# A four-layer graph network on a sparse matrix: diagonal terms moved from TensorE to ScalarE and VectorE, the short block first, column sums in the middle of layer 1

## The chip, the core and the metric

The kernel runs on one core of a Trainium2 chip. Its engines are TensorE (PE, matrix products; PEld are its weight loads), VectorE (DVE), ScalarE (ACT), GpSimd (POOL) and SyncE (SP), each with its own instruction queue that is worked off in order. The metric is the device time of one execution in microseconds (us).

## The reference, cut to what matters

x is 2708 x 512, adj is 2708 x 2708 and sparse: about four entries a row beside the diagonal, which is always there. Four layers follow each other, each in the form x = layernorm(x + layer(x, adj)):

```python
# layer 0
layer0 = (x - (adj @ x) * (diag + 1)) @ W0 + b0
# layer 1: gates ga, gb = sigmoid([adj @ x, x] @ Wa.T + ba), the same with Wb, bb
h = x @ W_sa
e = where(adj != 0, exp(-leaky_relu(s_left + s_right)), 0)
attn = e / (sum(e, axis=1) + 1e-5)
layer1 = sigmoid(ga * (attn @ h) + gb * (adj @ (x @ W_gc) + b_gc))
# layer 2: head = (adj > 0) / norm of its rows
inc = adj + head
layer2 = (inc @ x) / sum(inc, axis=1)
# layer 3: A = adj + I, deg = column sums of A, d = deg ** -0.5
layer3 = tanh((d[:, None] * A * d[None, :]) @ x @ W3.T + b3)
```

## The kernel before, in words

The 2708 nodes make 22 blocks of 128 rows; the last one, block 21, has 20 rows. Layer 0 reads adj once, block by block, and finds the entries beside the diagonal of every 128 columns (at most 8 in a segment of some blocks). It turns them into a list of edges: a full block has 5 tiles of 128 edges, the short one 1 tile (TILES, `n_tiles`). What is kept of them is ev (values, with the diagonal's value behind the last tile), ej and er (the node at either end), and pick, a 0/1 matrix per tile that says which row of the block an edge belongs to. A dense path stands behind a flag and isn't taken here.

Each later layer aggregates a block like this: GpSimd gathers the 5 x 128 neighbour rows from DRAM with indirect DMAs (L599, one per tile, tile xg, two buffers, in layer 1 also sl, a few columns of the row's own node). Then TensorE sums them up (`aggregate`, L656). A tile can be summed in two ways:

- *As an f32 product:* VectorE multiplies pick by the edge values (`weighted_edges`, L620), and TensorE multiplies the result with xg.
- *Split:* ScalarE scales the gathered rows by the edge values into a rounded fp32r tile hi (L641), VectorE computes the remainder lo (L643), and TensorE multiplies pick with hi and with lo. The rings of hi and lo have n_parts buffers each.

SPLIT_A, SPLIT_E and SPLIT_3 say how many of the 5 tiles are split in layer 1's two sums and in layer 3's; the others go as f32 products, and layer 2 splits none. The first product of every aggregate is the diagonal term: ScalarE scales the identity by the diagonal's values (`weighted_diagonal`, L629), and TensorE multiplies it, f32, with the block's own rows xs.

Layer 1 has two aggregates a block, l1a (by adj) and l1e (by the attention's weights). Its finish scales them by the gates into ua (L1213) and ue (L1215) on ScalarE, transposes both on TensorE (L679), copies them to SBUF on ScalarE (L684), and projects them with two weights into one accumulator, 8 f32 products (L692). Then follow L1222 on VectorE, a tanh on ScalarE (L1226), the residual (L1227), the norm (with a square root by Newton steps on VectorE, L718 to L737, and the scaling on ScalarE, L740), and the store to DRAM. Layer 3's finish scales its aggregate on ScalarE (L1360), transposes, projects with 4 products, and goes on in the same way from L1365; layer 2's has no projection (L1324).

Layer 0's order is written out by hand (`steps`, `plan`): each step has a time within a block, and blocks follow each other every 15.81 planned us, by block number. Outside it the tile framework orders the instructions of each engine from the program's order and its own cost model; `layer` gives the program's order as gather(i+1), prepare(i+1), then compute(i), with finish(i-1) between l1a and l1e. A layer's first gather reads rows that the layer before stored, so it waits for that layer's last store.

Ahead of layer 1 stand the column sums of adj for layer 3 (L1255 to L1279): a loop over five blocks of VectorE rows over 128 x 880 elements, some small rows, and a Sqrt on ScalarE (L1275). Behind layer 1 stands a second Sqrt, for layer 2's row norm (L1286). In layer 2 the prepared weights are two VectorE passes (L1310, L1318) over 6 x 128 columns: five tiles and the diagonal.

Of the kernel before, what the change touches and what calls it, by code (L numbers as in the profile page):

```python
# [12 lines left out]
P = 128  # L13
# [427 lines left out]

SPLIT_A, SPLIT_E, SPLIT_3 = 5, 3, 4

# [44 lines left out]
def sparse_path(  # L488
# [18 lines left out]
    def rows(i):  # L507
        return P if i < NF else TAIL

    def n_tiles(i):  # L510
        return TILES if i < NF else 1

    keep = outer.enter_context(tc.tile_pool(name="keep", bufs=1))
# [76 lines left out]
    d_inv = const.tile([P, NB], FP, name="d_inv")  # L590
    dd3 = const.tile([P, NB], FP, name="dd3")
    vsum = const.tile([P, NB], FP, name="vsum")
# [34 lines left out]
    def weighted_diagonal(s, i, v):  # L627
        r = rows(i)
        nc.scalar.activation(s[:, n_tiles(i), :r], ident[:, :r], AF.Copy, scale=v)  # L629

    def weighted(i, vals, pool, name, diag=None, first=0):
        nt = n_tiles(i)
        s = pool.tile([P, TILES + 1, P], FP, tag="s", name=name)
        weighted_edges(s, i, vals, first)
        weighted_diagonal(s, i, vals[:, nt : nt + 1] if diag is None else diag)
        return s
# [11 lines left out]
    def picked(pool, i):  # L648
# [5 lines left out]
        return s  # L654

    def aggregate(pool, i, s, tiles, tag, name, pick_s=None, parts=()):  # L656

        r = rows(i)
        nt = n_tiles(i)
        agg = pool.tile([P, D], FP, tag=tag, name=name)  # L660
        products = [(s[:, nt, :r], xs[:, i, :D])]
        products += [(s[:, t, :r], tiles[:, t, :D]) for t in range(len(parts), nt)]
        products += [(pick_s[:, t, :r], x_) for t, pair in enumerate(parts) for x_ in pair]
        for k, (w, x_) in enumerate(products):
            nc.tensor.matmul(  # L665
                agg[:r, :], lhsT=w, rhs=x_, start=k == 0, stop=k == len(products) - 1
            )
        return agg
# [45 lines left out]
    def rsqrt(y, a, r, name):  # L714

        k = small.tile([P, 4], FP, tag="newton", name=f"nw_{name}")
        bits = small.tile([P, 1], U32, tag="bits", name=f"bits_{name}")
        nc.vector.tensor_scalar(  # L718
            bits[:r, :], a.bitcast(U32), 1, None, op0=ALU.logical_shift_right
        )  # L720
        y0, t, y1, q = (k[:r, j : j + 1] for j in range(4))
        nc.vector.tensor_scalar(
            y0.bitcast(U32), bits[:r, :], -1.0, float(GUESS), op0=ALU.mult, op1=ALU.add
        )
        nc.vector.scalar_tensor_tensor(t, y0, a, y0, op0=ALU.mult, op1=ALU.mult)
        nc.vector.scalar_tensor_tensor(t, t, -10.0 / 3.0, t, op0=ALU.add, op1=ALU.mult)
        nc.vector.scalar_tensor_tensor(y1, t, 5.0, y0, op0=ALU.add, op1=ALU.mult)
        nc.vector.scalar_tensor_tensor(q, y1, a, y1, op0=ALU.mult, op1=ALU.mult)
        nc.vector.scalar_tensor_tensor(q, q, -64.0 / 3.0, y1, op0=ALU.add, op1=ALU.mult)
        nc.vector.tensor_scalar(y, q, -27.0 / 1024.0, None, op0=ALU.mult)  # L730

    def layernorm(dst, v, r, name):
# [355 lines left out]
    )  # L1088
    plan = [(i * STEP + s[0], i, s[1], s[2:]) for i in range(NB) for s in steps]
    plan.append((40, 0, lambda i: score_weights(), ()))  # L1090
    with tc.manual_schedule():
        for _, i, step, more in sorted(plan, key=lambda e: e[:2]):
            step(i, *more)

# [39 lines left out]

    n_parts = 9

# [5 lines left out]
    def l1_prepare(i, tiles):  # L1142
# [50 lines left out]

        g = w1p.tile([P, 3], FP, tag="g", name=f"g{i}", bufs=3)
        nc.vector.tensor_add(g[:r, 0:2], sums[:r, 3:5], xs[:r, i, D + 4 : D + 6])
# [5 lines left out]
        nc.vector.reciprocal(g[:r, 2:3], g[:r, 2:3])  # L1201
        nc.vector.tensor_mul(g[:r, 2:3], g[:r, 2:3], g[:r, 0:1])
        na, ne = min(nt, SPLIT_A), min(nt, SPLIT_E)
        parts_a = [split_rows(w1p, tiles, t, ev[:, i, t : t + 1], f"a{i}") for t in range(na)]
        parts_e = [split_rows(w1p, tiles, t, e[:, 2, t : t + 1], f"e{i}") for t in range(ne)]
        sv = weighted(i, ev[:, i], spool, f"s1v{i}", first=na)
        se = weighted(i, e[:, 2], w1p, f"s1e{i}", first=ne)
        return sv, se, g, picked(w1p, i), parts_a, parts_e

    def l1_finish(i, g, agg_a, agg_e):  # L1210
        r = rows(i)
        ua = work.tile([P, D], FP, tag="u", name=f"l1ua{i}")
        nc.scalar.activation(ua[:r, :], agg_a[:r, :], AF.Copy, scale=g[:r, 1:2])  # L1213
        ue = work.tile([P, D], FP, tag="xb", name=f"l1ue{i}")
        nc.scalar.activation(ue[:r, :], agg_e[:r, :], AF.Copy, scale=g[:r, 2:3])  # L1215
        uaT = transposed(psl, ua, r, f"l1a{i}")
# [15 lines left out]

    def layer(src, width, prepare, compute):

        nxt = gather(0, src, width)
        ready = prepare(0, nxt)
        done = None
        for i in range(NB):
            tiles = nxt
            nxt = gather(i + 1, src, width) if i + 1 < NB else None  # L1240
            ready_next = prepare(i + 1, nxt) if i + 1 < NB else None
            done = compute(i, tiles, ready, done)
            ready = ready_next
        done()

    def l1_compute(i, tiles, ready, finish_before):
        sv, se, g, pick_s, parts_a, parts_e = ready
        agg_a = aggregate(psl, i, sv, tiles, "agg", f"l1a{i}", pick_s, parts_a)
        if finish_before is not None:
            finish_before()  # L1250
        agg_e = aggregate(psl, i, se, tiles, "agg", f"l1e{i}", pick_s, parts_e)
        return lambda: l1_finish(i, g, agg_a, agg_e)


    deg = w1p.tile([P, NB], FP, name="deg", bufs=1)  # L1255
    block = w1p.tile([P, NB, SLOTS], U32, name="block", bufs=1)
    nc.vector.tensor_scalar(block, index, 7, None, op0=ALU.logical_shift_right)
    part = w1p.tile([P, NB, SLOTS], FP, name="deg_part", bufs=1)
    dsum = w1p.tile([P, len(SEGS)], FP, name="dsum", bufs=1)
    for m in range(max(hi - lo for lo, hi in SEGS)):  # L1260
        nc.vector.scalar_tensor_tensor(
            part, block, float(m), value, op0=ALU.is_equal, op1=ALU.mult
        )
        nc.vector.tensor_reduce(
            dsum, part.rearrange("p i (s k) -> p s i k", k=8), AX.XY, ALU.add
        )
        for s, (lo, hi) in enumerate(SEGS):
            if lo + m < hi:
                nc.vector.tensor_copy(deg[:, lo + m : lo + m + 1], dsum[:, s : s + 1])
    nc.vector.scalar_tensor_tensor(deg, dval, 1.0, deg, op0=ALU.add, op1=ALU.add)  # L1270

    zero = w1p.tile([P, NB], FP, name="zero", bufs=1)
    nc.vector.tensor_scalar(zero, deg, 0.0, None, op0=ALU.is_equal)
    nc.vector.tensor_add(d_inv, deg, zero)
    nc.scalar.activation(d_inv, d_inv, AF.Sqrt)  # L1275
    nc.vector.reciprocal(d_inv, d_inv)
    nc.vector.tensor_scalar(zero, zero, -1.0, 1.0, op0=ALU.mult, op1=ALU.add)
    nc.vector.tensor_mul(d_inv, d_inv, zero)
    nc.vector.scalar_tensor_tensor(dd3, dval, 1.0, d_inv, op0=ALU.add, op1=ALU.mult)  # L1279

    layer(x1d, XW, l1_prepare, l1_compute)


    inv_norm = const.tile([P, NB], FP, name="inv_norm")
    nc.vector.tensor_scalar(inv_norm, cnt, 1e-24, None, op0=ALU.max)
    nc.scalar.activation(inv_norm, inv_norm, AF.Sqrt)  # L1286
    nc.vector.reciprocal(inv_norm, inv_norm)
    nc.vector.tensor_mul(cnt, cnt, inv_norm)
    nc.vector.tensor_add(vsum, vsum, cnt)
    nc.vector.reciprocal(vsum, vsum)  # L1290
    p1.close()

# [6 lines left out]
    def l2_prepare(i, tiles):  # L1299
        r = rows(i)  # L1300
        m = n_tiles(i) + 1
        sp = ps2.tile([P, P], FP, tag="s", name=f"in_ps{i}")
# [18 lines left out]
    def l2_finish(i, agg):  # L1321
        r = rows(i)
        v = w2p.tile([P, D], FP, tag="v", name=f"l2v{i}")
        nc.vector.scalar_tensor_tensor(  # L1324
            v[:r, :], agg[:r, :], vsum[:r, i : i + 1], xs[:r, i, :D], op0=ALU.mult, op1=ALU.add
        )
# [23 lines left out]
    def l3_prepare(i, tiles):  # L1350
        nt = n_tiles(i)
        n3 = min(nt, SPLIT_3)
        parts = [split_rows(w3p, tiles, t, ev[:, i, t : t + 1], f"s{i}") for t in range(n3)]
        s = weighted(i, ev[:, i], spool, f"s3_{i}", diag=dd3[:, i : i + 1], first=n3)
        return s, picked(w3p, i), parts

    def l3_finish(i, agg):
        r = rows(i)
        u = work.tile([P, D], FP, tag="u", name=f"l3u{i}")
        nc.scalar.activation(u[:r, :], agg[:r, :], AF.Copy, scale=d_inv[:r, i : i + 1])  # L1360
        uT = transposed(ps3, u, r, f"l3_{i}")
# [55 lines left out]
```

## Time and profile before

| What | us |
|---|---|
| median of 14 runs | 1198.96 (1190.53 to 1204.99) |
| the profiled execution | 1195.03 |
| its span, first to last instruction | 1193.3 |
| mean granted TensorE clock | 0.93 |
| busy: PE, DVE, POOL, ACT | 967.6, 857.1, 711.6, 520.1 |
| layer 0 ends (last store of x1d issued) | 411 |
| layer 1: first gather, first L1222, last L1222 | 414, 483, 804 |
| layer 2: first gather, last store issued | 812, 979 |
| layer 3: first gather, last L1365 | 981, 1182 |

The page cuts the span into 40 slices of 29.8 us; a digit is the busy share of one engine in one slice, in tenths, and PEclk is the clock granted to TensorE:

```profile
PE   0268888988889626999999999997698855989995
DVE  3899999999984354677776777735578754778885
ACT  2334444444432134566665666631112214556662
POOL 5366656676674177577777766006777737666620
PEclk9998899999989756999999999998998976999998
```

The dips at slices 14 to 16, 28 to 29 and 33 to 34 are the passages from one layer to the next: there TensorE waits for the first gathers. Between them, in layers 1 and 3, its row is full of nines, while layer 0 has them in VectorE's row. Busy TensorE times are modelled and overlap, so what a matmul costs is read from the starts of neighbouring instructions.

### The profile page before, as it was taken

To read this page: it belongs to the slowest core of one execution; us is meant where nothing else is said; L and a number is where in the kernel's file an instruction comes from. 1 tells how busy PE (TensorE), PEld (TensorE's weight loads), DVE (VectorE), ACT (ScalarE), POOL (GpSimd) and SP (SyncE) were. 2 spreads that over 40 slices of the span, in tenths; PEclk is the share of its full clock that TensorE was granted. 3 is DMA by queue.
4 is the path that set the end of the run, shared out by engine and by line. 5 is a ranking of instruction groups with operands and counts; after the bars stand their busy time and mean duration, and the time that the engine had idled before them with its cause. 6 is when DMAs were issued, how large, how long until landed. Compare 5 with 4: busy or idle time off the path is not lost.

```text
span 1193.3 us, 12795 instructions
## 1 busy us (share of the span) xinstructions
PE 967.6 (81%) x3074; PEld 498.2 (42%) x3074; DVE 857.1 (72%) x2683; ACT 520.1 (44%) x1033; POOL 711.6 (60%) x765
## 2 busy tenths in 40 slices
PE   0268888988889626999999999997698855989995
PEld 0235444555445212555554555532233312545552
DVE  3899999999984354677776777735578754778885
ACT  2334444444432134566665666631112214556662
POOL 5366656676674177577777766006777737666620
PEclk9998899999989756999999999998998976999998
DMA  8466667666632222333333333014566635556621
GB/s 209 137 183 190 190 191 201 191 190 189 182 92 64 74 66 68 83 85 86 92 92 85 89 84 94 30 51 123 167 200 175 191 112 157 151 153 173 174 84 39
DMA packets 119690, 154.74 MB, mean 130 GB/s; under 512 B 24679, under 2 KB 82864, under 8 KB 119608
## 3 DMA queue, kind: packets, MB, share of 16 engines
q0 software_dynamic: 39024, 96.43, 30.1%
q1 hardware_dynamic: 78472, 57.42, 16.1%
q8 instruction: 26, 0.43, 0.1%
q14 instruction: 56, 0.46, 0.1%
q10 hardware_dynamic: 2112, 0.01, 0.1%
HBM read 153.55 MB, written 22.53 MB: 148 GB/s over the span
## 4 chain that ended last, share of the span: by engine, by line
PE 30%; DVE 18%; issue 9%; DMA 6%; ACT 3%; POOL 3%; another core or an unknown queue 2%; POOLq 0%; DVEq 0%; ACTq 0%
PE l1o L692 10%; PE l1e L665 5%; DMA xg<-x2d,ej 4%; PE l3o L692 3%; PE l2a L665 3%; DVE lo_a L643 3%; DVE lo_e L643 2%; POOL xg L599 2%; DVE lo_s L643 2%; PE l3a L665 2%; PE l0o L692 2%; DVE st_l L702 1%; PE l0a L1008 1%; PE l1a L665 1%
## 5 line engine op out<-in xcount | busy, mean ns | idle before, releaser
L599 POOL DMA_INDIRECT xg<-x1d,ej x106 | 114.5, 1080 | 66.3 <-PE l1e L665 40.7
L599 POOL DMA_INDIRECT xg<-in_x_dram,ej x106 | 115.2, 1087 | 52.0 <-issue 20.6
L599 POOL DMA_INDIRECT sl<-cold,er x106 | 125.5, 1184 | 34.4 <-issue 26.2
L599 POOL DMA_INDIRECT xg<-x3d,ej x106 | 111.6, 1053 | 56.3 <-issue 20.4
L599 POOL DMA_INDIRECT xg<-x2d,ej x106 | 116.0, 1095 | 46.8 <-issue 20.7
L665 PE MATMUL l2a<-xg,s2i 128*128 128x512 f32 x212 | 108.7, 636 | 14.1 <-DMA xg<-x2d,ej 12.2
L1008 PE MATMUL l0a<-xg,s 128*128 128x512 f32 x212 | 109.3, 617 | 0.0
L692 PE MATMUL l3o<-w_sb,uT_l 128*128 128x512 f32 (+1 forms) x176 | 85.3, 630 | 15.5 <-ACT uT_l L684 15.0
L692 PE MATMUL l1o<-w_gc_sb,uT_l1a 128*128 128x512 f32 (+1 forms) x176 | 88.5, 629 | 9.6 <-issue 5.9
L643 DVE SCALAR_TENSOR_TENSOR lo_s<-xg,ev,hi_s 128x512 fp32r<-128x512 f32 x85 | 63.2, 747 | 36.9 <-ACT hi_s L641 14.8
L692 PE MATMUL l0o<-w_sb,uT_l 128*128 128x512 f32 (+1 forms) x176 | 82.3, 611 | 0.4 <-ACT uT_l L684 0.4
L863 DVE FIND_INDEX8 index<-found,adj 128x8 uint32<-128x512 f32 (+1 forms) x110 | 81.3, 739 | 0.0
L862 DVE MAX8 found<-adj 128x8 f32<-128x512 f32 (+1 forms) x110 | 81.1, 737 | 0.0
L692 PE MATMUL l1o<-w_sa_sb,uT_l1e 128*128 128x512 f32 (+1 forms) x176 | 80.3, 599 | 0.0
L643 DVE SCALAR_TENSOR_TENSOR lo_a<-xg,ev,hi_a 128x512 fp32r<-128x512 f32 x106 | 78.1, 737 | 0.2 <-ACT hi_a L641 0.2
L641 ACT ACTIVATE hi_a<-xg,ev 128x512 fp32r<-128x512 f32 x106 | 69.7, 711 | 10.8 <-DMA xg<-x1d,ej 9.4
L665 PEld LDWEIGHTS l2a<-xg,s2i 128*128 128x128 f32 x212 | 38.8, 199 | 82.9 <-DMA xg<-x2d,ej 50.8
L913 PE MATMUL got<-found,sel 128*128 128x120 f32 x212 | 38.2, 343 | 42.2 <-DVE sel L902 42.1
L641 ACT ACTIVATE hi_s<-xg,ev 128x512 fp32r<-128x512 f32 x85 | 58.5, 712 | 22.2 <-DMA xg<-x3d,ej 14.9
L1222 DVE SCALAR_TENSOR_TENSOR l1v<-bg_bc,g,l1o 128x512 f32<-128x512 f32 (+1 forms) x22 | 16.4, 747 | 70.7 <-PE l1o L692 67.8
L847 ACT ACTIVATE minus<-adj 128x1408 bf16<-128x1408 f32 x44 | 60.6, 1377 | 14.9 <-POOL adj L842 14.1
L980 POOL TENSOR_SCALAR pick<-iota_c,ec 128x128 bf16<-128x128 f32 x106 | 62.5, 604 | 2.2
(235 smaller groups left out, 2158.0 us busy)
## 6 DMA issues: line engine op xcount, KB each, us to landing
adj<-in_adj_dram SPq DMA_DIRECT2D x21, 1344.0 KB
x1d<-xs SPq DMA_DIRECT2D x21, 264.0 KB
xs<-in_x_dram SPq DMA_DIRECT2D x21, 256.0 KB
x2d<-xs SPq DMA_DIRECT2D x21, 256.0 KB
x3d<-l2y SPq DMA_DIRECT2D x21, 256.0 KB
out_dram<-y SPq DMA_DIRECT2D x21, 256.0 KB
xg<-in_x_dram,ej POOLq DMA_INDIRECT x106
xg<-x1d,ej POOLq DMA_INDIRECT x106
```

The lines of the kernel that those rows point to most:

```text
L599: nc.gpsimd.indirect_dma_start(out=dst, out_offset=None, in_=src[:, :], in_offset=bass.IndirectOffsetOnAxis(ap=index, axis=0), bounds_chec ...
L641: nc.scalar.activation(hi, tiles[:, t, :D], AF.Copy, scale=v)
L643: nc.vector.scalar_tensor_tensor(lo, tiles[:, t, :D], v, hi, op0=ALU.mult, op1=ALU.subtract)
L665: nc.tensor.matmul(agg[:r, :], lhsT=w, rhs=x_, start=k == 0, stop=k == len(products) - 1)
L692: nc.tensor.matmul(o[:r, :], lhsT=uT[:, f, :r], rhs=w[:, f, :], start=start and f == 0, stop=stop and f == DB - 1,)
L847: nc.scalar.activation(minus, abuf[i % 2][:, k * half : (k + 1) * half, :], AF.Relu, scale=-1.0, accum_out=neg[:, i, k : k + 1],)
L862: nc.vector.max(out=best, in_=part)
L863: nc.vector.max_index(index[:, i, 8 * s : 8 * s + 8], best, part)
L913: nc.tensor.matmul(got[i][:, t // per_bank, k : k + 3 * SLOTS], lhsT=sel[i][:, t * P : (t + 1) * P], rhs=found[i].rearrange("p a s -> p (a ...
L980: nc.gpsimd.tensor_scalar(pick[:, i, t, :], iota_c, ec[:, t : t + 1], None, op0=ALU.is_equal)
L1008: nc.tensor.matmul(agg[i][:r, :], lhsT=weights[i][:, t, :r], rhs=rhs, start=t == 0, stop=t == nt)
L1222: nc.vector.scalar_tensor_tensor(v[:r, :], bg_bc[:r, :], g[:r, 1:2], o[:r, :], op0=ALU.mult, op1=ALU.add)
```

## The change

- The diagonal product leaves every aggregate of layers 1 to 3. In its place ScalarE scales the block's own rows (`scaled_rows`, 128 x 512, a coefficient per row), and VectorE adds them in the instruction that scales the aggregate. In layer 1 that is a new instruction for ua and ue each, in layer 3 for u, each in place of a ScalarE copy; in layer 2 an instruction of this form stood there already. Layer 1's copies are made in prepare, those of layers 2 and 3 in finish.
- SPLIT_E goes from 3 to 4, SPLIT_3 from 4 to 3, n_parts from 9 to 8.
- All layers take the short block first (SEQ), layer 0's plan too: the plan's times go by place in SEQ, not by block number.
- The column sums become `column_sums`, which stands in the program's order behind the compute of the twelfth block of layer 1.
- Both Sqrts outside layer 0 become Newton steps on VectorE (`rsqrt_columns`).
- Layer 2's two passes cover 5 x 128 columns instead of 6 x 128; its own coefficient own2 is computed ahead of it, layer 3's own3 in `column_sums`.

```diff
-SPLIT_A, SPLIT_E, SPLIT_3 = 5, 3, 4
+SPLIT_A, SPLIT_E, SPLIT_3 = 5, 4, 3
...
+    SEQ = ([NF] if TAIL else []) + list(range(NF))
...
+    def scaled_rows(pool, i, c, name):
+        r = rows(i)
+        t = pool.tile([P, D], FP, tag="own", name=name, bufs=3)
+        nc.scalar.activation(t[:r, :], xs[:r, i, :D], AF.Copy, scale=c)
+        return t
...
-        products = [(s[:, nt, :r], xs[:, i, :D])]
-        products += [(s[:, t, :r], tiles[:, t, :D]) for t in range(len(parts), nt)]
+        products = [(s[:, t, :r], tiles[:, t, :D]) for t in range(len(parts), nt)]
...
+    def rsqrt_columns(pool, y, a, n, name):
+        bits = pool.tile([P, n], U32, name=f"bits_{name}", bufs=1)
+        nc.vector.tensor_scalar(bits, a.bitcast(U32), 1, None, op0=ALU.logical_shift_right)
...
-    plan = [(i * STEP + s[0], i, s[1], s[2:]) for i in range(NB) for s in steps]
+    plan = [(k * STEP + s[0], k, s[1], s[2:]) for k in range(NB) for s in steps]
...
-        for _, i, step, more in sorted(plan, key=lambda e: e[:2]):
-            step(i, *more)
+        for _, k, step, more in sorted(plan, key=lambda e: e[:2]):
+            step(SEQ[k], *more)
...
-    n_parts = 9
+    n_parts = 8
...
+        nc.vector.tensor_mul(g[:r, 3:5], g[:r, 1:3], e[:r, 0:3:2, nt])
+        own = [scaled_rows(w1p, i, g[:r, k : k + 1], f"own{k}_{i}") for k in (3, 4)]
...
-        nc.scalar.activation(ua[:r, :], agg_a[:r, :], AF.Copy, scale=g[:r, 1:2])
+        nc.vector.scalar_tensor_tensor(
+            ua[:r, :], agg_a[:r, :], g[:r, 1:2], own[0][:r, :], op0=ALU.mult, op1=ALU.add
+        )
...
-        nc.scalar.activation(ue[:r, :], agg_e[:r, :], AF.Copy, scale=g[:r, 2:3])
+        nc.vector.scalar_tensor_tensor(
+            ue[:r, :], agg_e[:r, :], g[:r, 2:3], own[1][:r, :], op0=ALU.mult, op1=ALU.add
+        )
...
+    def layer(src, width, prepare, compute, aside=None):
+        nxt = gather(SEQ[0], src, width)
+        ready = prepare(SEQ[0], nxt)
         done = None
-        for i in range(NB):
+        for k, i in enumerate(SEQ):
...
+            if aside is not None and k == NB // 2:
+                aside()
...
-    layer(x1d, XW, l1_prepare, l1_compute)
+    layer(x1d, XW, l1_prepare, l1_compute, column_sums)
...
+        own = scaled_rows(w2p, i, own2[:r, i : i + 1], f"own_l2_{i}")
+        nc.vector.scalar_tensor_tensor(
+            v[:r, :], agg[:r, :], vsum[:r, i : i + 1], own[:r, :], op0=ALU.mult, op1=ALU.add
         )
...
-        nc.scalar.activation(u[:r, :], agg[:r, :], AF.Copy, scale=d_inv[:r, i : i + 1])
+        own = scaled_rows(w3p, i, own3[:r, i : i + 1], f"own_l3_{i}")
+        nc.vector.scalar_tensor_tensor(
+            u[:r, :], agg[:r, :], d_inv[:r, i : i + 1], own[:r, :], op0=ALU.mult, op1=ALU.add
+        )
```

## The prediction

> **What bounds the kernel now.** I read the busy time by stretches first (columns: span of the stretch, then busy us and instructions per engine, granted TensorE clock, DMA share, GB/s), then the waits inside layer 1, the groups by line and form, and the timeline of one block.
>
> ```profile
> 520.00:620.00 100.00, 98.85 (x346) 53.83 (x345) 74.31 (x308) 63.90 (x133) 73.55 (x65) 1.00 0.34 91
> 830.00:960.00 130.00, 107.74 (x230) 40.05 (x228) 94.79 (x301) 24.57 (x51) 98.13 (x90) 0.96 0.63 182
> 1060.00:1140.00 80.00, 78.26 (x245) 41.68 (x244) 68.69 (x205) 52.24 (x93) 53.40 (x52) 1.00 0.61 170
> ```
>
> The engines stand in the order PE, PEld, DVE, ACT, POOL. Layer 1 (first row) and layer 3 (third) are bound by TensorE, which is 98 to 99% busy at full clock. Layer 2 isn't: POOL is busy 98 of 130 us, and 90 pauses of 0.30 us between its gathers fill 27 more.
>
> ```profile
> DVE l1v L1222 <- PE l1o L692: 51.1, 17, 4.3
> POOL xg L599 <- PE l1e L665: 31.1, 31, 5.1
> POOL sl L599 <- issue: 18.3, 60, 0.3
> ACT hi_e L641 <- PE l1e L665: 7.6, 16, 0.5
> ```
>
> These are layer 1's waits from 505 to 790 us (us in total, times, longest). Everybody waits for PE; the gathers wait for it about 1.7 us a block. In layer 2 it is the other way round:
>
> ```profile
> PEld l2a L665 <- DMA xg<-x2d,ej: 44.6, 46, 2.0
> POOL xg L599 <- issue: 18.9, 62, 0.3
> ```
>
> Prices come from the groups by form, and from one stretch of timeline:
>
> ```profile
> L599 POOL DMA_INDIRECT sl<-cold,er x106 | 125.5, 1184 | 34.4 <-issue 26.2 <-DVE nw_l L725 3.4 <-DVE e L1159 2.3
> L599 POOL DMA_INDIRECT xg<-x1d,ej x106 | 114.5, 1080 | 66.3 <-PE l1e L665 40.7 <-issue 14.6 <-DVE lo_e L643 6.7
> L643 DVE SCALAR_TENSOR_TENSOR lo_e<-xg,e,hi_e 128x512 fp32r<-128x512 f32 x64 | 45.7, 740 | 5.9 <-ACT uT_l1e L684 4.1 <-PE l1e L665 1.8
> L1324 DVE SCALAR_TENSOR_TENSOR l2v<-l2a,vsum,xs 128x512 f32<-128x512 f32 x21 | 15.6, 742 | 12.3 <-PE l2a L665 11.5 <-PE in_ps L1303 0.8
> L641 ACT ACTIVATE hi_e<-xg,e 128x512 fp32r<-128x512 f32 x64 | 44.0, 718 | 14.5 <-PE l1e L665 10.2 <-DVE dsum L1264 2.3 <-DVE e L1163 0.2
> L629 ACT ACTIVATE s1v<-ident,ev 128x128 f32<-128x128 f32 x21 | 8.4, 400 | 4.0 <-PE l1a L665 2.7 <-PE l0a L1008 1.3
> ...
> 542.35 0.19 PEld L692 LDWEIGHTS l1o<-w_sa_sb,uT_l1e 128*128 128x128 f32 x1 [0.24 <-issue]
> 542.78 0.19 PEld L692 LDWEIGHTS l1o<-w_sa_sb,uT_l1e 128*128 128x128 f32 x1 [0.24 <-issue]
> ...
> 547.11 0.40 PE L665 MATMUL l1e<-hi_e,pick 128*128 128x512 f32 x1
> 547.34 0.40 PE L665 MATMUL l1e<-lo_e,pick 128*128 128x512 f32 x1
> ```
>
> One f32 instruction takes TensorE 0.43 us (542.35 to 542.78) and a product is two, 0.86 us; a split pair takes 2 x 0.23 = 0.47 us (547.11 to 547.34). These starts, not the modelled busy times, are PE's prices.
>
> **Layer 1, per full block.** The period is (794.84 - 482.98)/20 = 15.6 us between the L1222 rows of blocks 0 and 20. PE loses two diagonal products (1.72) and has a pair in place of a product (0.39): 15.4 busy becomes 13.3. DVE now does ua and ue, in the form of the L1324 row (2 x 0.74), one more lo_e (0.74) and a small multiply (0.16), and a smaller s1e (0.41 to 0.28 by the rows of both sizes): 74.31 x 0.156 = 11.6 becomes 13.8. ACT loses two diagonals (0.8) and two copies (1.34), gains two scaled copies (some 0.7 each) and a hi_e (0.72): no change at 10. POOL needs 5 x 1.18 + 5 x 1.08 + 10 x 0.30 = 14.3 as before.
>
> So the period can't fall by PE's 2.1 us. Its lower bound is 14.3, POOL's queue. Its upper bound is DVE's 13.8 with all of DVE's present idle time, 4.0 us, added: 17.8. Most of that idle is the wait for l1o (51.1 us in 17), which a shorter PE sequence takes away; the 0.8 us behind the tanh stay. ua and ue are new waits of DVE on PE: behind them in DVE's queue stand the lo rows, and PE's transposes wait for them; ACT did this before. I add 0.4 and choose 13.8 + 0.8 + 0.4 = 15.0, 0.6 less than now, 20 times: **-12** (-26 to +44). The ring of hi and lo buffers shrinks from 9 to 8 while a block now makes 9 pairs, so the last hi_e waits for the next l1a's first pair; some 7 us of projections cover that.
>
> In the trace's gathers after 410 us, 98 that ran beside a lo row alone took 1.22 us, against 1.01 for 122 beside no wide DVE row; 5 beside L1324 took 1.01. One more lo_e therefore makes POOL's bound 14.5, and ua and ue cost it nothing.
>
> [...]
>
> **Column sums.** They are ten rows of 1.06 us, a shift of 0.62, 22 copies and some 12 small rows: 15 us of DVE. Now they stand in layer 1's fill, where three of the 1.06 us rows and a Sqrt table load of 1.28 us fall into the first block's score chain (430 to 446 us): 4 us back at most. In mid-layer they cost 0 if DVE's idle time takes them, 15 if DVE is the bound; I take 6 for its 1.2 us of slack a block. Net **+2** (-4 to +15). The Sqrt at the layer's end went beside PE work: nothing.
>
> **The short block first.** In layer 1 it stands last today, L1222 at 794.84 for block 20 and at 803.75 for the short one: 8.9 us of nearly bare projections leave the end. At the start they fit while block 0's ten gathers (13 us) run. The last store is 256 KB instead of 40; the landing that gather 0 waits for grows by perhaps 1.5 us (estimate: the short x1d store landed in 2.2, a gather of a full tile takes 3 to 4). **-7.4** (-10 to +3). In layer 0 the last slot becomes a full one: at that end full slots are 11.1 to 11.3 us apart and the short one follows after 9.6 (L1066 rows), so 1.6, plus 1.5 for the store; in front, the 2.1 us clearing on POOL now precedes the first mask, but the first block's short gathers and picks give about that back. **+3** (0 to +8). Layer 3: L1365 at 1178.25 and 1182.07, 3.8 us less, 1.3 more for the store: **-2.5**. Layer 2's last full block ends where the short one did, with the larger store: **+1.5**.
>
> **Layer 2.** PE loses 0.86 a block, DVE's two s2i rows shrink by a sixth (-0.3), ACT gets a scaled copy for a diagonal (+0.3). The gathers run back to back: 1.09 + 0.30 = 1.4 each, 7.0 of a 7.2 us period. Only the 10 us of waits on l2a can go, and the new copy can come late in the finish: I take **-3** (-8 to +3).
>
> **Layer 3.** The period is 7.9 us (L1365 rows at 1095.09 and 1102.99). PE loses 0.86 and gains 0.39 from one split less: 7.7 busy (78.26 x 7.9/80) becomes 7.2. DVE gets u (+0.74), loses a lo_s (-0.75), and s grows by 0.13: 6.8 (68.69 x 7.9/80) becomes 6.9. ACT falls by 1.1. The bound below is PE's 7.2; above, 6.9 with DVE's present idle 1.1 a block is 8.0, and the new u may add 0.2. I take 7.5, halfway between 7.2 and 7.9, 20 times: **-8** (-14 to +6).
>
> Sum: -12 + 2 - 7.4 + 3 - 2.5 + 1.5 - 3 - 8 = -26.4. The profiled execution took 1195.0 us (span 1193.3), so it would become 1168.6; the runs' median lies 3.9 us higher, so I predict 1172.5.
>
> **Rivals.** *DVE takes over layer 1 (slower).* The new ua and ue stand in DVE's order between lo rows; if DVE keeps 3.2 us of waits a block, the period is 17.0, +28 in place of -12: 1212. It decides from a period of 16.3 (15.0 + 26.4/20), 2.5 us of DVE waits. For it: 13.8 of 15.6 is 88%, and DVE waits 4.0 now. Against it: three quarters of those are waits for PE.
>
> *Everything falls in place.* Layer 1 runs at POOL's 14.4 (-24), the sums hide in full (-4), layer 3 runs at 7.2 (-14), the rest as forecast: -50, so 1148.5. For it: POOL's only long wait is PE.
>
> *The freed TensorE time goes nowhere.* Ring, DVE order and gathers hold layers 1 and 3 at their periods; only the ends count: 2 - 7.4 + 3 - 2.5 + 1.5 - 3 = -6.4, so 1192.5. PE would then show idle time before l1a or the transposes.
>
> **Chances.** Forecast (1157 to 1188) 0.44; in place 0.17; nowhere 0.18; DVE takes over 0.21. A measurement of this kernel tells 0.3% (3.6 us) from no change. The first two are faster; of the third 0.11 faster, 0.06 same, 0.01 slower; of the fourth 0.02 same, 0.19 slower. The range 1148 to 1208 leaves out about half of the second and of the fourth case.
>
> **What would show it.** In the profile after: L1222 rows 15.0 us apart, DVE 90% busy in layer 1 and PE below 92%; xg gathers nearly without waits on l1e; no Sqrt row after layer 0; gathers of layer 2 still 1.4 us apart; L1365 rows 7.5 apart; no 20-row block at any layer's end. L1222 rows over 16.3 us apart, with idle DVE before ua or ue, would prove me wrong.

## The result: slower, and the profile after

The changed kernel takes 1239.51 us in the median (1229.03 to 1243.54, 10 runs); runs of the kernel before beside it took 1199.4 (47 runs). The ratio is 1.0334, with an interval of 1.0308 to 1.0361. The forecast was 1172.5, and the range ended at 1208. The profiled execution took 1236.6 us, its span is 1234.9.

Where the 41.6 us between the two spans came from, by the first gather of each layer and the rows of `l1v` (L1222 before, L1254 after):

| Stretch | before | after | difference | forecast |
|---|---|---|---|---|
| up to layer 1's first gather | 414.4 | 422.2 | +7.8 | +3 |
| from there to block 0's `l1v` | 68.6 | 77.0 | +8.4 | 0 |
| 20 intervals, block 0 to block 20 | 311.9 | 355.3 | **+43.4** | -12 |
| from there to layer 2's first gather | 17.0 | 8.8 | -8.2 | -7.4 |
| layer 2 | 169.5 | 167.8 | -1.7 | -1.5 |
| layer 3 and the end | 211.9 | 203.9 | -8.0 | -10.5 |

(The +2 for the column sums stands in no row; they are taken up below.) One term failed by far: layer 1's intervals. The stretches of the changed kernel that answer to the three of the prediction, in the same columns (PE, PEld, DVE, ACT, POOL, clock, DMA share, GB/s):

```profile
520.00:620.00 100.00, 80.92 (x259) 43.88 (x258) 71.46 (x269) 52.74 (x103) 61.41 (x55) 0.86 0.27 70
885.00:1010.00 125.00, 94.54 (x190) 32.43 (x190) 86.11 (x293) 29.56 (x50) 96.71 (x88) 0.96 0.63 183
1100.00:1180.00 80.00, 74.33 (x226) 38.90 (x225) 69.74 (x211) 44.89 (x72) 57.05 (x53) 0.98 0.59 173
```

In layer 1 (first row) no engine is full any more: TensorE 81%, DVE 71%, POOL 61%, and TensorE's granted clock has gone from 1.00 to 0.86. What holds the stage is then a chain of waits. Layer 1's waits after the change, 520 to 820 us (us in total, times, longest):

```profile
DVE q L1174 <- DMA xg<-x1d,ej: 83.3, 16, 6.4
...
PE l1o L699 <- ACT uT_l1a L691: 49.6, 16, 4.2
...
POOL sl L602 <- DVE e L1184: 41.6, 14, 4.4
POOL xg L602 <- PE l1e L672: 31.3, 16, 5.2
```

Every engine waits for another, each once a block. The timeline of one block shows in what order (start, duration, engine, line; idle time before it and its releaser in brackets):

```profile
592.58 0.39 PE L672 MATMUL l1e<-lo_e,pick 128*128 128x512 f32 x1
...
599.38 2.07 PE L699 MATMUL l1o<-w_gc_sb,uT_l1a 128*128 128x512 f32 x2 [3.69 <-ACT uT_l1a L691]
...
601.43 4.53 PE L699 MATMUL l1o<-w_gc_sb,uT_l1a 128*128 128x512 f32 x6
...
603.40 0.74 DVE L1245 SCALAR_TENSOR_TENSOR l1ue<-l1e,g,own 128x512 f32<-128x512 f32 x1
...
605.79 0.60 PE L686 MATMUL tr_l1e<-ident,l1ue 128*128 128x128 f32 x4
...
606.23 1.02 PE L672 MATMUL l1e<-xg,s1e 128*128 128x512 f32 x2
...
607.09 3.68 PE L699 MATMUL l1o<-w_sa_sb,uT_l1e 128*128 128x512 f32 x8
...
607.53 1.00 POOL L602 DMA_INDIRECT xg<-x1d,ej  x1 [2.34 <-PE l1e L672]
...
610.14 0.17 DVE L1174 COPY q<-xg 128x15 f32<-128x15 f32 x1 [4.88 <-DMA xg<-x1d,ej]
...
610.79 0.99 POOL L602 DMA_INDIRECT sl<-cold,er  x1 [2.26 <-DVE e L1184]
```

The aggregate l1e is complete at 593.0, but ue, which scales it, starts at 603.40, **10.4 us later**, and DVE stood idle for only 0.42 us in between (ahead of the small `sum` row at 601.62). All that hangs on ue is late with it: its transposes, the next block's l1e, whose first product needs the PSUM buffer that ue has just read, GpSimd's last xg gather, which needs the tile that this product read, the landing of that gather, and `q`, which stands in DVE's queue ahead of `l1v`, of the next sl gather's releaser and of everything that makes the next block's parts.

Before, the same step took 0.7 us, on ScalarE (548.19 to 548.92), and the second transposes came right behind the first, ahead of the w_gc projection:

```profile
547.80 0.39 PE L665 MATMUL l1e<-lo_e,pick 128*128 128x512 f32 x1
...
548.92 0.67 ACT L1215 ACTIVATE l1ue<-l1e,g 128x512 f32<-128x512 f32 x1
...
551.65 0.60 PE L679 MATMUL tr_l1e<-ident,l1ue 128*128 128x128 f32 x4
```

The compiled order of DVE's rows in one block of the changed kernel (wide rows and `q` alone) says why. l1ue is the block's own finish; the lo rows, s1e and pick ahead of it belong to blocks further on, whose prepare stands earlier in the program:

```
l1v | lo_a_4 lo_e_0 lo_e_1 lo_e_2 lo_e_3 | l1v+xs | lo_a_0 .. lo_a_3 | s1e pick | l1ue l1ua | q ... l1v
```

### The profile page after: what moved, and what is told of

Same layout as the page of the kernel before. It is cut to its first block, busy times and chain, and to the rows that moved or that the text cites. A ratio compares the mean times of both kernels' runs of the same rounds, so it can differ in the third digit from the quotient of the medians.

```text
span 1234.9 us, 12495 instructions
## 1 busy us (share of the span) xinstructions
PE 932.7 (76%) x2898; PEld 480.1 (39%) x2898; DVE 896.2 (73%) x2790; ACT 505.2 (41%) x961; POOL 726.3 (59%) x765
## 3 DMA queue, kind: packets, MB, share of 16 engines
q0 software_dynamic: 39024, 96.43, 28.7%
q1 hardware_dynamic: 78472, 57.42, 15.6%
## 5 line engine op out<-in xcount | busy, mean ns | idle before, releaser
L602 POOL DMA_INDIRECT sl<-cold,er x106 | 129.2, 1219 | 79.1 <-DVE e L1184 50.3
L699 PE MATMUL l1o<-w_gc_sb,uT_l1a 128*128 128x512 f32 (+1 forms) x176 | 125.0, 853 | 58.0 <-ACT uT_l1a L691 58.0
L602 POOL DMA_INDIRECT xg<-x3d,ej x106 | 116.4, 1099 | 50.6 <-issue 22.9
L602 POOL DMA_INDIRECT xg<-x2d,ej x106 | 119.4, 1126 | 45.0 <-issue 27.1
L672 PE MATMUL l2a<-xg,s2i 128*128 128x512 f32 (+1 forms) x212 | 116.0, 669 | 38.5 <-DMA xg<-x2d,ej 21.8
L1033 PE MATMUL l0a<-xg,s 128*128 128x512 f32 (+1 forms) x212 | 109.2, 616 | 0.0
L1174 DVE COPY q<-xg 128x15 f32<-128x15 f32 (+1 forms) x22 | 3.8, 175 | 109.4 <-DMA xg<-x1d,ej 109.4
L699 PEld LDWEIGHTS l1o<-w_gc_sb,uT_l1a 128*128 128x128 f32 (+1 forms) x176 | 42.1, 265 | 102.1 <-ACT uT_l1a L691 62.7
L672 PEld LDWEIGHTS l2a<-xg,s2i 128*128 128x128 f32 (+1 forms) x212 | 37.9, 203 | 112.7 <-DMA xg<-x2d,ej 52.2
L872 ACT ACTIVATE minus<-adj 128x1408 bf16<-128x1408 f32 x44 | 60.6, 1377 | 19.8 <-POOL adj L791 15.7
L699 PEld LDWEIGHTS l3o<-w_sb,uT_l 128*128 128x128 f32 (+1 forms) x176 | 33.7, 199 | 69.6 <-issue 38.6
```

Source lines behind the costliest of these rows:

```text
L602: nc.gpsimd.indirect_dma_start(out=dst, out_offset=None, in_=src[:, :], in_offset=bass.IndirectOffsetOnAxis(ap=index, axis=0), bounds_chec ...
L672: nc.tensor.matmul(agg[:r, :], lhsT=w, rhs=x_, start=k == 0, stop=k == len(products) - 1)
L699: nc.tensor.matmul(o[:r, :], lhsT=uT[:, f, :r], rhs=w[:, f, :], start=start and f == 0, stop=stop and f == DB - 1,)
L872: nc.scalar.activation(minus, abuf[i % 2][:, k * half : (k + 1) * half, :], AF.Relu, scale=-1.0, accum_out=neg[:, i, k : k + 1],)
L1033: nc.tensor.matmul(agg[i][:r, :], lhsT=weights[i][:, t, :r], rhs=rhs, start=t == 0, stop=t == nt)
```

## The experiments

The runs of one group shared a chip; each ratio is against runs of the kernel before beside it (1199.4 us for the first row, 1191 to 1193 us for the others, on the chip of e9 to e12 1174.39, so their microseconds stand only beside each other). "Interval" is the mean distance of the 20 `l1v` rows from block 0 to 20 (15.6 before, 17.8 after; 18.4 in mid-layer, since the last two blocks of the changed kernel, with little beside them, are 12.8 and 11.2 apart).

| Run | What differs | Ratio (95%) | Interval |
|---|---|---|---|
| after | the change | 1.033 (1.031 to 1.036) | 17.8 |
| e1_split3 | after, 8 pairs in 8 buffers | 1.028 (1.022 to 1.034) | 17.6 |
| e2_ring9 | after, 9 pairs in 9 buffers | 1.031 (1.027 to 1.034) | 17.5 |
| e3_diag_pe | after, layer 1's diagonal on TensorE | 1.005 (1.002 to 1.008) | 15.9 |
| e4_before_ring | before, 9 pairs in 8 buffers | 1.007 (1.003 to 1.011) | 16.1 |
| e5_order | after, priority for ua and ue | 0.987 (0.981 to 0.992) | 15.1 |
| e6_order_ring | e5 with 8 pairs in 9 buffers | 0.987 (0.981 to 0.993) | 15.6 |
| e7_diag_ring | e3 with 8 pairs in 9 buffers | 0.986 (0.981 to 0.991) | 15.5 |
| e8_short_last | e7, short block last | 1.000 (0.997 to 1.003) | 15.6 |
| e9_dve_copies | before, ua and ue scaled on DVE | 1.024 (1.018 to 1.030) | 16.9 |
| e10_ue_first | after, priority for ue alone | 0.992 (0.989 to 0.995) | 15.0 |
| e11_warm | after, 14 idle products a block | 1.019 (1.013 to 1.025) | 16.7 |
| e12_sums_mid | e5, column sums really in mid-layer | 0.989 (0.983 to 0.995) | 15.5 |
| e13_ring9_diag | e3 with 9 pairs in 9 buffers | 1.003 (0.999 to 1.006) | 16.2 |
| e14_diag_mid | e13, column sums really in mid-layer | 1.005 (1.001 to 1.009) | 16.5 |

### The ring, or the place of ua and ue

Theory A blamed the shorter ring, theory B DVE's order.

```diff
e1   SPLIT_E = 3                    # n_parts stays 8
e2   n_parts = 9                    # SPLIT_E stays 4; s1e holds one tile
e3 + products = [(s[:, nt, :r], xs[:, i, :D])] + ...       # layer 1 only
e3 + nc.scalar.activation(ua[:r, :], agg_a[:r, :], AF.Copy, scale=g[:r, 1:2])    # ue alike
e4   SPLIT_E = 4, n_parts = 8       # in the kernel before
```

> The changed kernel with SPLIT_E back at 3, so that a block of layer 1 makes 8 pairs for its 8 buffers. Theory A (ring): nine pairs in a ring of eight make the parts of a block wait for the products of the one before; with 8 pairs the L1254 rows fall from 18.4 us apart to about 15.5 and the time to 1180 to 1195 us. Theory B (DVE's order): ue stands in DVE's order behind the next block's lo_a rows, s1e and pick, so its transposes, the w_sa projection and the first l1e product, which needs the buffer that ue frees, start late; the ring has no part in it, the period stays at 18.0 to 19.0 and the time at 1230 to 1250 us.

> The changed kernel with n_parts back at 9; to make room for it s1e holds only the one tile that is used of it. Theory A (ring): period about 15.5 us, time 1180 to 1195 us. Theory B (DVE's order): lo_a's last row only moves within DVE's order, ue stays where it is, period 17.5 to 18.5, time 1220 to 1240 us.

> The changed kernel with layer 1's two diagonal products back on TensorE and ua and ue back as ScalarE copies; the ring of 8 with 9 pairs, the short block first and the column sums in mid-layer stay. Theory A (ring): the period stays above 17.5 us and the time above 1225. Theory B (DVE's order): the two transposes stand together again, the period is 15.0 to 15.6 and the time 1175 to 1192 us.

> The kernel before with SPLIT_E 4 and n_parts 8 alone. Theory A (ring): period over 17.5 us, time over 1230 us. Theory B (DVE's order): a pair in place of an f32 product takes 0.39 us from TensorE a block, so the period is 15.0 to 15.7 and the time 1188 to 1203 us.

Theory A falls: neither a pair less nor a buffer more takes more than 0.3 us off the interval, and 9 pairs in 8 buffers, put into the kernel before, bring 0.7%, not 3.3%. With the diagonal and the copies of ua and ue back where they were, nearly all of it is gone: 1193.27 us, interval 15.9 (16.3 in mid-layer, as in e4); time and interval are a little above what B promised. So the loss lies in the diagonal's move, as B says, but e3 takes back two things at once: the products on TensorE, and the engine of ua and ue.

### Their order alone

```diff
e5 + with tc.high_priority():
         nc.vector.scalar_tensor_tensor(ua[:r, :], agg_a[:r, :], g[:r, 1:2], own[0][:r, :], ...)
         nc.vector.scalar_tensor_tensor(ue[:r, :], agg_e[:r, :], g[:r, 2:3], own[1][:r, :], ...)
e6   e5, SPLIT_E = 3, n_parts = 9
e10  e5 with the block around ue alone
```

> The changed kernel with ua and ue given priority in the framework's ordering and nothing else: DVE's order now has ue behind lo_e's first row instead of behind the next block's lo_a rows, s1e and pick, and ua of the next block right after lo_e's last row. The work, the ring of 8 and the 9 pairs stay. Theory B (DVE's order): the period falls from 18.4 us to the 16.3 of the two kernels with the diagonal on TensorE and a ring of 8, time 1188 to 1203 us. Theory C (DVE's load): the two rows of 0.74 us more on DVE cost the time wherever they stand, period 17.5 or more, time over 1220 us.

> The run before with SPLIT_E 3 and n_parts 9 as well (s1e holds the two tiles that are used of it). If the ring of 8 with 9 pairs costs 0.7 us a block, as the 16.3 us of the two kernels with the diagonal on TensorE say, the period is 15.0 to 15.7 and the time 1165 to 1185 us; if the ring has no part once the order is mended, it equals the run before within 4 us. Under theory C (DVE's load) the period stays above 17 us and the time above 1205.

> The changed kernel with priority for ue alone; ua keeps its low rank and stands near the end of DVE's block, just ahead of L1255. If ue's place decides (its transposes, the w_sa projection and the first l1e product wait for it), the period is under 15.8 us and the time 1175 to 1190 us, as with priority for both. If ua's place matters as much, since the next tr_l1a and w_gc wait for it, the period is over 16.5 us and the time over 1200.

The priority removes no work; it moves ue and ua forward in DVE's order, and the framework's order of the other engines follows. The kernel goes from 1.033 to 0.987, 1179.11 us, better than B promised, and ue's place alone does nearly all of it. Theory C (DVE's load) falls: the rows cost nothing where they stand right, with DVE busier than before (163.73 of the 200 us from 520 to 720, against 142.76). One block of e5:

```profile
571.43 0.40 PE L672 MATMUL l1e<-lo_e,pick 128*128 128x512 f32 x1
...
574.82 0.74 DVE L1246 SCALAR_TENSOR_TENSOR l1ue<-l1e,g,own 128x512 f32<-128x512 f32 x1
...
576.60 0.60 PE L686 MATMUL tr_l1e<-ident,l1ue 128*128 128x128 f32 x4
```

ue starts 3.0 us after the aggregate is done, and its transposes come 1.8 us behind it, ahead of both projections again. GpSimd's queue shows what that is worth. Its own waits from 520 to 720 us, after the change:

```profile
POOL sl L602 <- DVE e L1184: 29.7, 10, 3.5
POOL xg L602 <- PE l1e L672: 20.6, 11, 2.8
```

In e5 GpSimd waits for `e` 6.9 us in the same stretch, and for l1e not at all.

Ten gathers a block are 11.2 us (121.61 us busy over the 10.9 blocks of those 200 us) and ten pauses of 0.3, 14.2 in all; the changed kernel adds 4.6 us of these two waits (50.3 / 10.9) in place of two of the pauses: 18.2. The 14.2 is the prediction's lower bound, 14.3 by GpSimd's queue, and the interval is that plus what GpSimd waits for. Such an account says where the time lies, not why; the cause is shown by e5, which changes nothing but the priority of the two rows.

In e6 the pair less and the ninth buffer bring nothing more (1181.87 against 1179.11 us), so no sign is left that the ring costs time. (In the profiles e6's 20 intervals are longer, 311.9 against 301.1 us, and its fill, from the first gather to block 0's row, is shorter, 71.2 against 75.4.)

### Moving the copies alone

```diff
- nc.scalar.activation(ua[:r, :], agg_a[:r, :], AF.Copy, scale=g[:r, 1:2])
+ nc.vector.tensor_scalar(ua[:r, :], agg_a[:r, :], g[:r, 1:2], None, op0=ALU.mult)      # ue alike
```

> The kernel before with ua and ue scaled on VectorE instead of ScalarE and nothing else: the diagonal products stay on TensorE, 9 buffers, 8 pairs. The framework again puts ue behind the next block's lo rows and the second transposes behind the w_gc projection. Theory B (DVE's order): this alone brings the loss, L1222 rows 17.5 to 19.5 us apart and the time 1235 to 1275 us. Theory D (the framework needs the diagonal product as the aggregate's first one to order TensorE well): the period stays at 15.3 to 16.2 and the time at 1188 to 1207 us.

In the kernel before, with every diagonal product in place, this alone costs 28 us (1202.6 against 1174.39 on that chip), and the compiled order again has tr_l1e behind w_gc. Theory D falls (17.0 us apart in mid-layer, above its 16.2). But B promised 17.5 or more. What lies between 17.0 and 18.4 may be TensorE's clock, which stays at 1.00 in e9:

```profile
520.00:720.00 200.00, 179.90 (x624) 100.18 (x623) 144.01 (x574) 101.17 (x216) 132.69 (x118) 1.00 0.30 81
```

The changed kernel is granted 0.85 in the same stretch, with TensorE busy 165.1 of the 200 us. In e9 TensorE's gap ahead of w_gc is 0.99 us long (592.74 to 593.73), in the changed kernel 3.69.

### The clock

TensorE in one block of the changed kernel, in two stretches, the idle gap ahead of w_gc, and w_gc with the sums (span, PE busy, granted clock, DMA share, GB/s); on both sides of them the clock is 1.00.

```profile
595.70:599.38 3.68, 0.00 (x0) 0.82 0.08 7
599.38:606.00 6.62, 6.62 (x15) 0.58 0.45 119
```

After 3.68 us without work the next 6.62 us run at a clock of 0.58: by an estimate from these two numbers 2.8 us are lost (6.62 x 0.42); two instructions of w_gc take 2.07 us where eight of w_sa take 3.68 a little later. The gap is there because of another engine's order: w_gc waits for the copy `uT_l1a` on ScalarE, which is busy 3.63 of the 3.68 us and does a tanh and four hi_a rows first, though the transposes that the copy needs ended at 595.69:

```profile
595.80 0.61 ACT L1258 ACTIVATE l1v<-l1v 128x512 f32<-128x512 f32 x1
596.32 2.54 ACT L642 ACTIVATE hi_a<-xg,ev 128x512 fp32r<-128x512 f32 x4
...
598.77 0.56 ACT L691 COPY uT_l1a<-tr_l1a 128x512 f32<-128x512 f32 x1
```

In e9 the same four rows run from 590.46 to 593.01, beside l1a's products, and the copy follows 0.37 us behind the transposes. e11 fills the gap with work that nobody needs:

```diff
+ for _ in range(14):      # behind l1a's products
+     nc.tensor.matmul(warm[:r, :], lhsT=pick_s[:, 0, :r], rhs=parts_a[-1][1], start=True, stop=True)
```

> The changed kernel with 14 more split products a block right behind l1a's, into a PSUM tile that nobody reads: 14 x 0.23 = 3.3 us of TensorE work in the 3.7 us in which it stood idle ahead of the w_gc projection. Theory E (the granted clock): the 6.6 us that followed the gap at a clock of 0.58 shrink to about 3.8 us, the period falls from 18.4 to 15.6 to 16.6 us and the time to 1180 to 1205, though there is more work. Rival: the loop through DVE and the gathers sets the period whatever the clock, it stays at 18.0 or more and the time at 1230 or more.

The same stretch of e11, in the columns of the whole row, and its longest wait of GpSimd:

```profile
520.00:720.00 200.00, 191.20 (x732) 118.42 (x731) 153.41 (x582) 113.30 (x220) 124.81 (x116) 1.00 0.31 84
```

```profile
POOL xg L602 <- PE l1e L672: 25.0, 11, 4.6
```

Fourteen useless products a block make the kernel 1.4% faster than without them: the clock stays at 1.00, w_gc's eight instructions take 3.9 us instead of 6.6, the rows are 17.1 us apart in mid-layer. It is between the two expectations: the clock is a part of the loss, and the wait of the gathers for l1e (25.0 us in 11) is still there. How much exactly is the clock's stays open, since the added products also moved `q` forward in DVE's order.

### The other parts of the change

```diff
e7   e3, SPLIT_E = 3, n_parts = 9
e8   e7, SEQ = list(range(NB))
e13  e3, n_parts = 9
e12, e14 + with tc.issue_after(last_v[0]):    # the l1v row that compute(11) has just traced
               aside()
```

> The changed kernel with layer 1's diagonal on TensorE, SPLIT_E 3 and n_parts 9: layer 1's work of a block as before the change; the short block first, the column sums in mid-layer and layers 2 and 3 as changed. If the ring costs 0.7 us a block, the period is 15.6 as before and the time 1174 to 1186 us, the sum of what the other parts of the change bring. If the 16.3 us came from the short block first or the column sums, the time stays at 1190 to 1197.

> The run before with the short block last again in all layers. By the terms of the prediction (-7.4 in layer 1, +3 in layer 0, -2.5 in layer 3, +1.5 in layer 2) it is 5.4 us slower than that run. If the short block's order costs in layer 0 what the changed kernel shows there (+7.5 at the last x1 columns) and layer 1 gains only the end, it is the same or up to 4 us faster.

> The changed kernel with layer 1's diagonal on TensorE and n_parts 9, SPLIT_E still 4: against the run with the diagonal on TensorE and 8 buffers (period 16.3 us, ratio 1.005) only the ring differs. Theory F (ring): the ninth buffer lets lo_a's last row be made earlier, so the lo_e rows, for which GpSimd's gathers wait 1.6 us a block there, come earlier too; the period falls to 15.0 to 15.7 us and the ratio to 0.980 to 0.990. Rival: the ninth pair itself, a lo row more ahead of the gather that waits, costs the 0.7 us; the period stays at 16.0 to 16.4 and the ratio at 1.000 to 1.008.

e13 tells what the 16.3 us were: not the ring (theory F falls, 16.5 us apart in mid-layer with 9 buffers) but the ninth pair, SPLIT_E 4. Against e7 it costs 14.4 us in 20 intervals (323.4 against 309.0). GpSimd waits for the lo_e rows 11.6 us in 200, against 5.6 in e7, but for l1e 17.9 against 23.4, so its waits do not explain the loss, and by what path the pair costs stays open. This is e13's row for lo_e:

```profile
POOL xg L602 <- DVE lo_e L646: 11.6, 11, 1.1
```

e7 against e8 is the short block: 1178.81 against 1194.14 us, more than the 5.4 of the prediction. The profiled executions are further apart, 24.5 us (e8's took 1202.67 us, 8.5 above its median); 17.4 of them lie in layer 1, of which 8.3 are the end and 6.9 the fill (66.0 against 72.8 us from the first gather to block 0's row). The fill is no firm gain: it lasts 66.0 to 77.5 us in the kernels with the short block first and 61.6 to 72.8 in those with it last. Layer 0 shows nothing over all kernels: layer 1 begins at 415.8 to 423.7 us with it first, at 414.4 to 427.3 with it last.

> The run with priority for ua and ue, with the column sums held behind the twelfth L1257 row in DVE's order: in all kernels so far the framework drew them forward into layer 1's fill, wherever they stand in the program. If DVE's idle time takes their 15 us in mid-layer and the fill gets shorter by 4 us, it is 2 to 6 us faster than that run (1173 to 1177 us); if DVE is close to the bound, the 15 us come back in mid-layer and it is 4 to 10 us slower (1183 to 1189).

> The run before with the column sums held behind the twelfth L1254 row in DVE's order, which is where the change meant to have them. With the diagonal on TensorE, DVE is busy 72% in mid-layer. If the sums hide there and the fill gets shorter by the 5.7 us that the other run with them in mid-layer showed, it is 3 to 7 us faster than the run before, the fastest kernel of this study against the kernel before (0.975 to 0.985). If mid-layer pays them in full, as with ua and ue on DVE, it is 0 to 8 us slower than the run before.

The column sums were the part of the change that did not do what it says. They stand behind the twelfth block's compute in the program, but their operands are ready from the start, and the framework placed them in layer 1's fill, where they stood before the change too (412.1 to 435.0 us then, 420.7 to 478.7 now). Rows of the changed kernel, then of e14, which holds them back (first and last start at the end of each list):

```profile
L1298 DVE SCALAR_TENSOR_TENSOR deg_part<-block,value x5: 1060/1067/1074, 420.7 to 466.4; 128x880 f32<-128x880 uint32 x5
```

```profile
L1299 DVE SCALAR_TENSOR_TENSOR deg_part<-block,value x5: 1060/1065/1077, 640.4 to 655.4; 128x880 f32<-128x880 uint32 x5
```

Held back they gain nothing: in e14 the fill stays (70.7 against 71.2 us) and the 20 intervals grow by 6.9 us; in e12 the fill gets 5.7 us shorter and the intervals grow by 9.8. Of the two outcomes weighed for each, the one without a gain came true.

## Why the prediction was wrong, point by point

- **The step that failed:** "behind them in DVE's queue stand the lo rows, and PE's transposes wait for them; ACT did this before. I add 0.4 and choose 13.8 + 0.8 + 0.4 = 15.0". The lo rows stand not behind ue but ahead of it. I took the program's order of a block for the engine's order, on an engine that the framework orders anew, by a rule that I had described myself: prepare of the next block stands ahead of finish in the program. In place of 15.0 us the mean interval became 17.8, 2.8 more, of which an unknown part is the clock's. With ue in its place 20 intervals take 301.1 us in e5 and 300.3 in e10, where the forecast was 300, but luck has a part in that: 6.7 of the 10.8 us that e5 is below the kernel before lie in the last two intervals (22.0 against 28.7 us), and the first 18 are 15.5 us apart against 15.7, not 15.0.
- **The rival** "DVE takes over" had the sign and the place, DVE's order, and its time, 1212, was too low. Its mechanism was another: it wanted idle DVE in front of ua and ue, which there isn't, and DVE at its bound, which is busy 70%. The sign "PE below 92%" was met (83% from 520 to 720 us), for the opposite reason; "DVE 90% busy" was not.
- **The clock** had no term. I priced TensorE's instructions at full clock, 0.43 us, and the freed time as free. TensorE's idle time collected in one gap of 3.68 us ahead of w_gc, behind ScalarE's hi_a rows, and the 6.62 us behind that gap ran at a clock of 0.58.
- **"a pair in place of a product (0.39)"** as a gain: wrong with the diagonal on TensorE (e13 against e7, 14.4 us lost), no gain in time with the order mended (e5 against e6). The ring: rightly set at nothing (e2 against the changed kernel, e13 against e3). One more lo_e on GpSimd's bound, 14.3 to 14.5: open, the gathers of a block take 11.2 us with it and 11.3 before (144.35 us over 12.8 blocks), but ten of them take 11.3 us in e13 and 11.1 in e7 (137.96 us for 122, 142.60 for 128), which differ by that row. Nor do all gathers beside a lo row take longer: in the trace before, 30 gathers beside a lo_s row and no other DVE row over 0.3 us took 1.03 us, 24 beside a lo_a row 1.45.
- **Column sums, +2:** not moved to mid-layer, only spread out in the fill; whether that has a part in the fill's 8.4 us more isn't shown. Moved in earnest, they cost more in mid-layer than the fill gives back, within the -4 to +15 of the prediction.
- **The short block, -7.4:** the end gave 8.2 us; "at the start they fit" is not borne out, since the fill grew by 8.4 in the changed kernel, in a range that moves from kernel to kernel. **Layer 0, +3:** +7.8 in this pair of profiles, but no difference over all kernels.
- **Layers 2 and 3:** -1.7 against -1.5, and -8.0 against -10.5. In layer 3 the 20 intervals are 7.4 us shorter in all (161.1 to 153.7; forecast 8). Layer 2's gathers are still 1.4 us apart (96.71 / 88 + 0.30), as forecast.

e5 and e7 both beat the kernel before by 1.3 to 1.4%: the change pays, either with ua and ue ranked, or without the diagonal's move in layer 1. That move itself brings nothing even when ranked: e6 has it, ranked, and e7 has not, both with 8 pairs in 9 buffers, and they take 1181.87 and 1178.81 us. In this the rival "the freed TensorE time goes nowhere" was right for layer 1.

## What to carry to other kernels

Where a framework orders the engines, moving an instruction to another engine also gives it a new rank there: read in the compiled order which rows stand ahead of it, and what waits for it, before its duration is counted. A part that is moved in the program may not move at all, or may move something else; the first look is where its rows start. When every engine is idle part of the time, look for the instruction whose operand was ready long before it ran, and give it priority before anything is taken back.

## What the runs showed of the hardware that was not expected

TensorE's idle gap ahead of w_gc cost twice in the changed kernel, as idle time and by the clock behind it. After 3.68 us of idle time the granted clock was 0.58 over the next 6.62 us. Cut more finely, it is 1.00 up to 598.05, 2.35 us into the gap, 0.50 from there to 604.88, and 1.00 again behind that. In e5, where TensorE's gaps between 560 and 590 us are 1.05 and 1.82 us, the clock is 1.00 there (0.97 over 520 to 720), and in e9 and e11 it is 1.00 over 200 us.

The length of a gap alone does not decide. In the changed kernel a gap of 2.46 us (615.33 to 617.79) is followed by a clock of 0.59 over 4.16 us; one of 2.85 us in its layer 0 (238.15 to 241.00) is followed by 1.00 over 4.30 us. What decides whether a gap lowers the clock is not shown.
